# Row entries by distance from the middle of a row's span, and two seams of layer 0 in another order

## The chip, the cores and the metric

The kernel runs on one core of one Trainium2 chip. The metric is device time in microseconds of one execution; a profile of one execution shows what each engine did in it. The engines are named as in the profile: PE is TensorE (PEld its weight loads), DVE is VectorE, ACT is ScalarE, POOL is GpSimd, SP is SyncE, which here only issues DMAs.

## The reference, cut to what matters

Four graph layers run over x, 32 batches of 512 nodes with 128 features, and one adjacency matrix adj of 512 by 512. Each layer normalises x, applies a relu and adds the layer's output to x. The change lies in layer 0:

```python
h = jnp.maximum(_layernorm(x, axis=-1), 0.0)
# _L0_gnn_ref(h, adj, W, e, bias):
h0 = jnp.einsum('bnf,fg->bng', input, W[0])
h1 = jnp.einsum('bnf,fg->bng', input, W[1])
m = adj > 0
idx = jnp.cumsum(m.reshape(-1).astype(jnp.int32)) - 1
vals = e[0][idx].reshape(adj.shape)
A = jnp.where(m, vals, jnp.float32(NEG))
A = jax.nn.softmax(A, axis=1)
M = jnp.eye(adj.shape[0], dtype=A.dtype)
out = jnp.einsum('ij,bjg->big', A * M, h0) + jnp.einsum('ij,bjg->big', A * (1.0 - M), h1)
return out + bias[None, None, :]
```

The edges of adj are numbered row by row. Edge number k takes the k-th value of e, which has 256 entries; every edge beyond takes the last one. So the kernel has to find, for each of the first 256 edge numbers, the row and column that it lies in. A softmax over each row gives the attention matrix, whose diagonal multiplies h W[0] and whose other entries multiply h W[1].

## The kernel before

**Tiling.** The 512 rows of adj are four tiles (t = 0 to 3) of 128 partitions. The 32 batches are 16 pairs, q = 0 to 15, and x of a pair is one tile of 128 partitions by 2 by 4 by 128. All layers run pair by pair.

**The order of the work.** From by_source on, the instructions of TensorE, VectorE, ScalarE and GpSimd keep the order in which the source emits them, engine by engine. The emission is interleaved by hand: helpers are Python generators that emit some instructions per step, and go(steps, n) takes n steps of one. An instruction that waits holds all that stands behind it on its engine. DMAs are issued by SP; those under keep_in_program_order keep their order there too.

**The front (0 to about 15 us).** m is adj > 0 and rc[p, t] the number of edges in a row (L519). p_incl, a triangle of ones times rc (L528), is the number of edges up to and including a row; incl is its copy and before is incl - rc. Then edge k belongs to a row if before <= k < incl. The loop over t at L552 makes of_row[:, t, k] for k = 0 to 255 with two VectorE instructions: lt is k < incl (L554), and of_row is (k >= before) * lt (L555). TensorE multiplies each t with m into p_row (L558); its two banks go to pgs, one on ScalarE (L569) and one on VectorE (L570). p_upto is pgs times the triangle (L602), and scr_c (L616) counts from it the column of each edge. at_row, at_col and at_part (L619 to L623) are one-hot matrices; score_rows multiplies them into the score and value of each row tile (L654, L658), and softmax_rows and scaled_rows finish the attention matrix.

Beside it the statistics of x run for the first pairs: bn_stats on VectorE (L229), sd, sh and rs on GpSimd (L233 to L237), and h on ScalarE (L313).

**The seams.** In layer 0 each pair q goes through: statistics; h (normalise, eight ACTIVATEs at L313); hT, the transpose of h; p_g = hT times W[1] (L446, project_steps); g_high, g_low and g_mid, three parts of it (L468 to L474); p_l, the attention matrix times the parts (L800, mixed) plus own_sums, hd times W[0] (L793), where hd is hT times the diagonal (L728, GpSimd); and added (L808), which adds p_l to x. bias(q) adds the layer's bias to x on GpSimd (L453). For q up to 2, TensorE transposes h. From q = 3 on, turn(q) does it: two block transposes on VectorE (hb_hT, L349), four DMAs to DRAM (d_hT, L356) and one back (hT, L358), all issued on SP.

first_sums covers pair 0 and prepares pairs 1 to 3. Its first seam is at its end, where bias(1) stands ahead of the end of ln3, the statistics of pair 3 (the last two steps of which are L259 and L260 on GpSimd, the shift that h of pair 3 waits for):

```python
        diagonal_of(1, 1)
        bias(1)
        go(ln3)
        for I in range(2):
            added(0, I, ps[I])
```

round0(q) is the round of each later pair; it projects pair q + 1, turns pair q + 3 and starts h of pair q + 4. In round 2 alone the projection of pair 3 comes after mixed(q, 0). There lies the second seam: go(steps) emits p_g's evictions, and bias(q + 1) follows it, both ahead of turn(q + 3), which is turn(5). Loads of x for later pairs (load_x, L135) follow at the end of odd rounds.

Of the kernel before, what the change touches and what calls it, by code (L numbers as in the profile page):

```python
# [9 lines left out]
F32 = mybir.dt.float32  # L10
# [3 lines left out]
AF = mybir.ActivationFunctionType  # L14
OP = mybir.AluOpType
AX = mybir.AxisListType

P = 128
# [11 lines left out]
def kernel(  # L30
# [37 lines left out]
    nc = tc.nc  # L68
    B, N, D = x.shape
    NT = N // P  # L70
    NE = e_l0.shape[1]
    NK = NE // P
    NQ = B // 2
# [10 lines left out]
    def bank(name):  # L84
        return psum.tile([P, 512], F32, tag="bank", name=name)
# [4 lines left out]
    def blk(t):  # L90
        return slice(t * P, (t + 1) * P)
# [56 lines left out]
    def spread(w, n):  # L148
        return w[:, None, :].to_broadcast([P, n, D])
# [32 lines left out]
    prep = prep_scope.enter_context(tc.tile_pool(name="prep", bufs=1))  # L182
# [4 lines left out]
    cols = prep.tile([P, N], F16, name="cols")  # L187
# [118 lines left out]
    def normed_tile(q):  # L306
        return work.tile([P, 2, NT, D], F32, tag="h", name=f"h_{q}", bufs=3)
# [36 lines left out]
    def turn_steps(h, name, done):  # L344


        hb = late.tile([P, NQR, 2, NT, QR], F32, tag="hb", name=f"hb_{name}", bufs=2)
        for b in range(2):
            nc.vector.transpose(hb[:, :, b].rearrange("p j t r -> p t j r"),  # L349
                                h[:, b].rearrange("p t (j c) -> p t j c", c=QR))  # L350
            yield
        d = bounce.tile([NQR, QR, NQR, 2 * P], F32, tag="d", name=f"d_{name}")
        hT = feature_major(name)
        held = tc.keep_in_program_order if name.startswith("hT0") else lambda step: step
        for i in range(NQR):
            held(nc.sync.dma_start(d[:, :, i, :].rearrange("j c e -> c j e"),  # L356
                                   hb[i * QR : (i + 1) * QR].rearrange("c j b t r -> c j (b t r)")))
        held(nc.sync.dma_start(hT.rearrange("p i b n -> p (i b n)"), d.rearrange("j c i e -> (j c) (i e)")))  # L358
        done[name] = hT
# [90 lines left out]
    def bias(q):  # L450

        for b in range(2):
            nc.gpsimd.tensor_add(xt[q][:, b], xt[q][:, b], spread(b0, NT))  # L453
# [23 lines left out]
    def go(steps, n=99):  # L477
        for _ in range(n):
            if next(steps, steps) is steps:
                return  # L480
# [32 lines left out]
    rc = prep.tile([P, NT], F32, name="rc")  # L513
# [8 lines left out]
    rch = prep.tile([P, NT], F16, name="rch")  # L522
    nc.vector.tensor_copy(rch, rc)

    pi = bank("p_incl")
    for t in range(NT):
        for s in range(t + 1):
# [11 lines left out]
        nc.tensor.matmul(scores[t], ident16, m[:, t, :], start=True, stop=False)  # L539
    early = [early_stats(0, (0, 2), (2, 4)), early_stats(1, (0, 4)), early_stats(2, (0, 4))]  # L540
    go(early[0], 2)
    incl = prep.tile([P, NT], F32, name="incl")
    nc.vector.tensor_copy(incl, pi[:, :NT])
    before = prep.tile([P, NT], F32, name="before")
    nc.vector.tensor_sub(before, incl, rc)
    h = {q: normed_tile(q) for q in range(3)}
    hT = {q: feature_major(f"hT0_{q}") for q in range(3)}
    normal = [normed_steps(q, h[q]) for q in range(3)]
# [1 line left out]
    of_row = prep.tile([P, NT, NE], F16, name="of_row")  # L550
    pg = [bank(f"p_row_{i}").rearrange("p (j k) -> p j k", j=2) for i in range(NT // 2)]
    for t in range(NT):  # L552
        s = prep.tile([P, NE], F16, tag="lt", name=f"lt_{t}", bufs=2)
        nc.vector.tensor_scalar(s, cols[:, :NE], incl[:, t : t + 1], None, OP.is_lt)  # L554
        nc.vector.scalar_tensor_tensor(of_row[:, t, :], cols[:, :NE], before[:, t : t + 1], s,  # L555
                                       OP.is_ge, OP.mult)
        for j in range(NT):
            nc.tensor.matmul(pg[j // 2][:, j % 2, :], m[:, t, blk(j)], of_row[:, t, :],  # L558
                             start=(t == 0 and j % 2 == 0), stop=(t == NT - 1), skip_group_check=True)
    go(early[0], 2)  # L560
    nc.vector.tensor_scalar(known[:, :, 0], before, float(NE), None, OP.min)
    pb = bank("p_known")[:, : 2 * NK].rearrange("p (k e) -> p k e", e=2)
    for kk in range(NK):
# [50 lines left out]
    for kk in range(NK):  # L614
        s = prep.tile([P, N], F16, tag="scr", name=f"scr_c{kk}", bufs=2)
# [109 lines left out]
    def straight(hT, b, scale, name):  # L725

        s = owns.tile([P, N], F32, tag="hs", name=name, bufs=6)
        nc.gpsimd.tensor_mul(split(s), hT[:, :, b, :].rearrange("p b (a c) -> p a b c", c=QR), split(scale))  # L728
        return s
# [30 lines left out]
    ln3 = stats_steps(3, apart=True)  # L760
# [7 lines left out]
    def turn(q):  # L768

        if q not in turning:  # L770
            turning[q] = turn_steps(h[q], f"hT0_{q}", hT)
        next(turning[q])
        return turning[q]

    def turned_of(q):
        return hT[f"hT0_{q}"] if q > 2 else hT[q]
# [4 lines left out]
    def diagonal_of(q, b):  # L781
        hd[q, b] = straight(turned_of(q), b, adiag[0], f"hd_{q}_{b}")
# [13 lines left out]
    def mixed(q, I, p, part, first):  # L796

        for i in range(2):
            for t in range(NT):
                nc.tensor.matmul(p[:, i * 2 * D : (i + 1) * 2 * D], att_parts[part][:, t, blk(2 * I + i)],  # L800
                                 g[q][part][:, t].rearrange("p b f -> p (b f)"),
                                 start=(first and part == 0 and i == 0 and t == 0), stop=(part == 2 and t == NT - 1),
                                 skip_group_check=True)
# [6 lines left out]
    def first_sums():  # L810


        adiag.append(region0.tile([P, N], F32, name="adiag", bufs=1))
        ps = opened_sums(0)
        mixed(0, 0, ps[0], 0, True)
        transpose_rows(pt, att, 2)
        transpose_rows(pt, att, 3)
        for j in range(NT):
            att_high(j, 1, True)
        go(normal[1])  # L820
        go(early[2], NT + 2)
        att_low(1)
        att_mid(1)
        mixed(0, 0, ps[0], 1, True)
        mixed(0, 0, ps[0], 2, True)
        p_adiag = bank("p_adiag")
        for t in range(NT):
            nc.tensor.matmul(p_adiag[:, blk(t)], ones, diag[:, t, :], start=True, stop=True)
        nc.scalar.copy(adiag[0], p_adiag)
        go(early[2])  # L830
        diagonal_of(0, 0)
        diagonal_of(0, 1)
        next(turned[1])
        mixed(0, 1, ps[1], 0, True)
        go(turned[1])
        go(normal[2], NT)
        go(ln3, NT)
        next(project[1])
        mixed(0, 1, ps[1], 1, True)
        mixed(0, 1, ps[1], 2, True)  # L840
        go(project[1])
        go(normal[2])
        go(ln3, 1)
        own_sums(0, ps, False)
        diagonal_of(1, 0)
        diagonal_of(1, 1)
        bias(1)
        go(ln3)
        for I in range(2):
            added(0, I, ps[I])  # L850
        next(turned[2])
        go(turned[2])
        normalise(3)
        diagonal_of(2, 0)
        diagonal_of(2, 1)
        go(ahead[4], NT)
        go(turn(3))
        go(ahead[4])
# [3 lines left out]
    def round0(q):  # L862

        more = q + 1 < NQ
        nothing = iter(())
        both = stats_of_two(q - 1, q + 5) if q + 5 < NQ else stats_steps(q - 1, apart=True)
        ps = opened_sums(q)
        own_sums(q, ps, True)
        normal_of = normals.pop(q + 3, nothing)
        go(normal_of)  # L870
        go(both, NT)
        if more:
            if q > 1:
                diagonal_of(q + 1, 0)
                diagonal_of(q + 1, 1)
            steps = projection(q + 1)
            if q != 2:
                next(steps)
                if q > 2:
                    bias(q + 1)  # L880
                go(steps)
        if q + 5 >= NQ:
            go(both)
        if q == 1:
            bias(2)
            normalise(4)
            go(ahead[5])
            h[5] = normed_tile(5)
            normals[5] = normed_steps(5, h[5])
        elif q + 4 < NQ:  # L890
            h[q + 4] = normed_tile(q + 4)
            normals[q + 4] = normed_steps(q + 4, h[q + 4])
            go(normals[q + 4], NT)
        if q >= 5:
            go(sums_ahead, 1)
        for part in range(3):
            mixed(q, 0, ps[0], part, False)
        if q == 2:
            go(steps)
            bias(q + 1)  # L900
        if q + 3 < NQ:
            go(turn(q + 3))
        go(both, NT + 1)
        added(q, 0, ps[0])
        go(both)
        if q in (3, 4):
            next(squares)
            next(squares)
        if q == 5:
            go(squares)  # L910
        for part in range(3):
            mixed(q, 1, ps[1], part, False)
        added(q, 1, ps[1])
        if q == NQ - 1:
            own[q] = stats_steps(q)
        if q % 2 and q // 2 + NQ // 4 < NQ // 2:
            loads(q // 2 + NQ // 4)
# [613 lines left out]
```

## Time and profile before

| | |
|---|---|
| median of 3 runs | 883.40 us (883.37, 883.40, 884.81) |
| profiled execution: its own time | 883.62 us |
| its span, first to last instruction | 881.8 us |
| busy PE, PEld | 870.2 us (99%), 771.3 us (87%) |
| busy DVE, ACT, POOL | 702.4 us (80%), 574.7 us (65%), 608.4 us (69%) |
| granted TensorE clock, mean | 0.997 |

The profiled execution lies 0.2 us above the median. Its span leaves out 1.8 us around the first and the last instruction. Busy shares are means over four layers with different limits; what a change to layer 0 is worth has to be read from the stretches in which it lies, which are 7 to 15 us for the row entries and 40 to 76 us for the seams. Matmul ends are modelled in a trace, so TensorE counts as busy in some of its short waits; the starts of the weight loads show them better.

### The profile page before, as it was taken

To read this page: it belongs to the slowest core of one execution; us is meant where nothing else is said; L and a number is where in the kernel's file an instruction comes from. 1 tells how busy PE (TensorE), PEld (TensorE's weight loads), DVE (VectorE), ACT (ScalarE), POOL (GpSimd) and SP (SyncE) were. 2 spreads that over 40 slices of the span, in tenths; PEclk is the share of its full clock that TensorE was granted. 3 is DMA by queue.
4 is the path that set the end of the run, shared out by engine and by line. 5 is a ranking of instruction groups with operands and counts; after the bars stand their busy time and mean duration, and the time that the engine had idled before them with its cause. 6 is when DMAs were issued, how large, how long until landed. Compare 5 with 4: busy or idle time off the path is not lost.

```text
span 881.8 us, 16286 instructions
## 1 busy us (share of the span) xinstructions
PE 870.2 (99%) x5520; PEld 771.3 (87%) x5520; DVE 702.4 (80%) x1428; ACT 574.7 (65%) x1279; POOL 608.4 (69%) x624
## 2 busy tenths in 40 slices
PE   8999999999999999999999999999999999999998
PEld 4799999988888888888888888888889988899987
DVE  8769877568587787888778888888789789988875
ACT  4765565355555656556666888875688788766674
POOL 5768988766777867867776566565476766677664
PEclk9999999999999999999999999999999999999999
DMA  9146664312322213122342445455445555555433
GB/s 262 29 133 182 194 186 120 97 49 73 101 68 73 72 48 96 49 72 72 97 120 77 116 134 136 138 152 146 134 123 141 157 156 159 151 143 147 128 100 86
DMA packets 107684, 103.91 MB, mean 118 GB/s; under 512 B 9552, under 2 KB 94160, under 8 KB 107600
## 3 DMA queue, kind: packets, MB, share of 16 engines
q1 hardware_dynamic: 107312, 102.34, 41.1%
q8 instruction: 44, 0.72, 0.4%
q10 hardware_dynamic: 288, 0.52, 0.2%
q14 instruction: 40, 0.33, 0.1%
HBM read 53.02 MB, written 49.81 MB: 117 GB/s over the span
## 4 chain that ended last, share of the span: by engine, by line
PE 90%; DVE 3%; ACT 2%; POOL 2%; DMA 1%; issue 1%; SPq 0%; POOLq 0%; ACTq 0%; DVEq 0%
PE p_av L1298 13%; PE p_l L990 10%; PE p_hidden L1194 10%; PE p_x1T L397 10%; PE p_score L1276 10%; PE p_l L800 8%; PE p_w L969 5%; PE p_l L446 3%; PE p_z L446 3%; PE p_w L971 3%; PE p_feat L1171 3%; PE p_hidden L1174 3%; PE p_g L446 2%; PE p_query L1230 2%; PE p_hv L1242 2%; PE p_l L793 2%
## 5 line engine op out<-in xcount | busy, mean ns | idle before, releaser
L1298 PEld LDWEIGHTS p_av<-hv,ex 128*128 128x128 f32 x1024 | 119.2, 191 | 3.0 <-POOL ex L1271 0.4
L1298 PE MATMUL p_av<-hv,ex 128*128 128x129 f32 x1024 | 119.7, 274 | 0.2 <-POOL ex L1271 0.2
L313 ACT ACTIVATE h<-x,sh,rs 128x128 f32<-128x128 f32 x256 | 102.9, 483 | 4.4 <-POOL sh L260 2.3
L427 POOL TENSOR_TENSOR key<-key 128x512 fp32r<-128x512 f32 x32 | 47.9, 1498 | 83.4 <-DVE key L426 66.5
L1271 DVE TENSOR_TENSOR ex<-ex,adjTx 128x512 f32<-128x512 f32 x64 | 79.0, 1237 | 32.4 <-ACT ex L1269 31.0
L1271 POOL TENSOR_TENSOR ex<-ex,adjTx 128x512 f32<-128x512 f32 x64 | 99.6, 1574 | 6.9 <-issue 3.5
L1100 ACT ACTIVATE h<-x,sh,rs 128x128 f32<-128x128 f32 x256 | 102.9, 485 | 0.0
L413 POOL TENSOR_TENSOR low_h<-h,high_h 128x512 fp32r<-128x512 f32 x32 | 55.3, 1732 | 45.6 <-PE p_w L971 26.3
L1277 ACT ACTIVATE ex<-p_score 128x512 f32<-128x512 f32 x128 | 76.2, 598 | 11.5 <-PE p_score L1276 4.7
L1269 ACT ACTIVATE ex<-ex 128x512 f32<-128x512 f32 x128 | 77.3, 634 | 0.0
L1158 POOL TENSOR_SCALAR high_hT<-hT 128x512 fp32r<-128x512 f32 x32 | 20.5, 641 | 56.0 <-PE p_hidden L1174 28.9
L246 DVE BATCH_NORM_STATS2 bn<-x 128x6 f32<-128x256 f32 x160 | 58.3, 419 | 0.0
L399 ACT COPY x1T<-p_x1T 128x512 f32<-128x512 f32 x32 | 18.8, 587 | 57.7 <-PE p_x1T L397 57.7
L1214 POOL TENSOR_TENSOR x<-x,phi2b 128x256 f32<-128x256 f32 x64 | 56.3, 900 | 0.0
L413 POOL TENSOR_TENSOR low_hs<-hs,high_hs 128x512 fp32r<-128x512 f32 x32 | 44.0, 1388 | 14.9 <-ACT high_hs L412 14.4
L1276 PE MATMUL p_score<-high_query,key 128*128 128x512 f32 x128 | 50.5, 394 | 0.0
L1276 PE MATMUL p_score<-mid_query,key 128*128 128x512 f32 x128 | 50.4, 394 | 0.0
L1276 PE MATMUL p_score<-low_query,key 128*128 128x512 f32 x128 | 50.4, 394 | 0.0
L431 ACT ACTIVATE high_query<-p_query 128x512 fp32r<-128x512 f32 x32 | 19.2, 600 | 46.5 <-PE p_query L1230 46.5
L971 PE MATMUL p_w<-th,x1T 128*128 128x128 f32 x256 | 49.0, 273 | 0.0
L414 DVE SCALAR_TENSOR_TENSOR mid_h<-h,high_h 128x512 fp32r<-128x512 f32 x32 | 27.7, 870 | 23.7 <-ACT high_h L412 16.2
L1109 DVE STREAM_TRANSPOSE hb<-h 128x512 f32<-128x512 f32 x64 | 43.5, 697 | 2.5 <-DMA d<-hb 1.9
(246 smaller groups left out, 2623.1 us busy)
## 6 DMA issues: line engine op xcount, KB each, us to landing
d<-hb SPq DMA_DIRECT2D x128, 128.0 KB, 2.4
hT<-d SPq DMA_DIRECT2D x32, 512.0 KB, 3.7
d_hT<-hb_hT SPq DMA_DIRECT2D x116, 128.0 KB, 2.4
hT<-d_hT SPq DMA_DIRECT2D x29, 512.0 KB, 3.3
x<-in_x_dram SPq DMA_DIRECT2D x32, 256.0 KB, 5.3
dv<-hvb SPq DMA_DIRECT2D x128, 64.0 KB, 1.8
hvt<-dv SPq DMA_DIRECT2D x32, 256.0 KB, 2.7
out_dram<-x SPq DMA_DIRECT2D x31, 256.0 KB, 2.5
```

What stands on the lines that cost most here:

```text
L313: nc.scalar.activation(h[:, b, t, :], xt[q][:, b, t, :], AF.Relu, bias=shift[q][:, i : i + 1], scale=scale[q][:, i : i + 1])
L397: nc.tensor.matmul(p, right[part][:, blk(t)], left[part][:, t, :], start=(t == 0 and part == 0), stop=(t == NT - 1 and part == 2))
L413: nc.gpsimd.tensor_sub(low, x, high.bitcast(F32))
L971: nc.tensor.matmul(p[:, D:], x1[q, b][:, blk(t)], th[:, 2, :], start=False, stop=True, skip_group_check=True)
L990: nc.tensor.matmul(p, adj_parts[part][:, t, blk(i)], w[r][part][:, t, :], start=(part == 0 and t == 0), stop=(part == 2 and t == NT - 1))
L1100: nc.scalar.activation(h[:, t, :], xt[q][:, b, t, :], AF.Relu, bias=shift[q][:, i : i + 1], scale=scale[q][:, i : i + 1])
L1194: nc.tensor.matmul(sums2[n], weighed_features[n][i][:, blk(t)], sq[i][:, t, :], start=False, stop=(i == 2 and t == NT - 1), skip_group_che ...
L1269: nc.scalar.activation(ex[:, t, :], ex[:, t, :], AF.Exp, scale=8.0)
L1271: eng.tensor_mul(split(ex[:, t, :]), split(ex[:, t, :]), crossed(mask[:, t, :]))
L1276: nc.tensor.matmul(p, keys[n][i][:, t, :], query[n][i], start=(i == 0), stop=(i == 2))
L1277: nc.scalar.activation(crossed(ex[:, t, :]), split(p), AF.Tanh, scale=UP / (8.0 * math.sqrt(D)))
L1298: nc.tensor.matmul(po[:, i, : D + 1], ex[:, t, blk(i0 + i)], hv[:, t, :], start=(t == 0), stop=(t == NT - 1))
```

## The change

**Row entries.** The span of a row, before to incl - 1, has its middle at incl - rc/2 - 1/2. An edge number k lies in the row if its distance from the middle is less than rc/2. On GpSimd, half = rc/2 and above = rc/2 + 1/2 are made once for all t. middle = above - p_incl (VectorE, read from PSUM) is the middle with its sign turned. For each t, ScalarE makes s = |k + middle| (an ACTIVATE of function Abs with a bias per partition), and VectorE makes of_row = s < half. The copy incl is gone, and before is made after the loop, from PSUM.

**Two seams.** In first_sums, go(ln3) now stands ahead of bias(1). In round0, turn(q + 3) now stands ahead of the projection's evictions of round 2; for other rounds the emission is the same.

TensorE's and SP's instructions keep their order. VectorE has four instructions fewer, ScalarE four more, GpSimd two more.

```diff
     rch = prep.tile([P, NT], F16, name="rch")
     nc.vector.tensor_copy(rch, rc)
 
+    half = prep.tile([P, NT], F32, name="half")
+    nc.gpsimd.tensor_scalar(half, rc, 0.5, None, OP.mult)
+    above = prep.tile([P, NT], F32, name="above")
+    nc.gpsimd.tensor_scalar(above, rc, 0.5, 0.5, OP.mult, OP.add)
+
...
     go(early[0], 2)
-    incl = prep.tile([P, NT], F32, name="incl")
-    nc.vector.tensor_copy(incl, pi[:, :NT])
-    before = prep.tile([P, NT], F32, name="before")
-    nc.vector.tensor_sub(before, incl, rc)
+    middle = prep.tile([P, NT], F32, name="middle")
+    nc.vector.tensor_sub(middle, above, pi[:, :NT])
...
         s = prep.tile([P, NE], F16, tag="lt", name=f"lt_{t}", bufs=2)
-        nc.vector.tensor_scalar(s, cols[:, :NE], incl[:, t : t + 1], None, OP.is_lt)
-        nc.vector.scalar_tensor_tensor(of_row[:, t, :], cols[:, :NE], before[:, t : t + 1], s,
-                                       OP.is_ge, OP.mult)
+        nc.scalar.activation(s, cols[:, :NE], AF.Abs, bias=middle[:, t : t + 1])
+        nc.vector.tensor_scalar(of_row[:, t, :], s, half[:, t : t + 1], None, OP.is_lt)
...
     go(early[0], 2)
+    before = prep.tile([P, NT], F32, name="before")
+    nc.vector.tensor_sub(before, pi[:, :NT], rc)
     nc.vector.tensor_scalar(known[:, :, 0], before, float(NE), None, OP.min)
...
         diagonal_of(1, 1)
+        go(ln3)
         bias(1)
-        go(ln3)
         for I in range(2):
...
             mixed(q, 0, ps[0], part, False)
+        if q + 3 < NQ:
+            go(turn(q + 3))
         if q == 2:
             go(steps)
             bias(q + 1)
-        if q + 3 < NQ:
-            go(turn(q + 3))
         go(both, NT + 1)
```

## The prediction

> **What bounds the kernel now.** I read the chain of waits first, then TensorE's own waits, then the timeline around each wait. The page's chain is TensorE nearly throughout, so a change counts only where TensorE stands still or where another engine feeds it late:
>
> ```profile
> PE 90%; DVE 3%; ACT 2%; POOL 2%; DMA 1%; issue 1%; SPq 0%; POOLq 0%; ACTq 0%; DVEq 0%
> ```
>
> Both seams lie in layer 0. TensorE's waits between 20 and 140 us (total us, times, longest) hold one DMA row, met twice:
>
> ```profile
> PE p_g L446 <- DMA hT<-d_hT: 1.5, 2, 1.2
> ```
>
> The timeline of weight loads (start, duration) shows their full price, because load starts have a fixed pitch: a part of eight p_l L800 matmuls starts 0.96 us after the last, and p_g L446 follows sixteen L793 loads after 1.80 us (62.61 to 64.41):
>
> ```profile
> 56.47 1.03 PEld L800 LDWEIGHTS p_l<-g_mid,att_mid 128*128 128x128 f32 x8
> 57.96 1.86 PEld L446 LDWEIGHTS p_g<-w,hT 128*128 128x128 f32 x16 [0.47 <-issue]
> ...
> 62.61 1.88 PEld L793 LDWEIGHTS p_l<-w,hd 128*128 128x128 f32 x16
> 64.41 1.87 PEld L446 LDWEIGHTS p_g<-w,hT 128*128 128x128 f32 x16
> ...
> 71.94 1.88 PEld L793 LDWEIGHTS p_l<-w,hd 128*128 128x128 f32 x16
> 75.22 1.86 PEld L446 LDWEIGHTS p_g<-w,hT 128*128 128x128 f32 x16 [1.40 <-DVE bn L272]
> ```
>
> p_g of batch pair 3 was due at 56.47 + 0.96 = 57.43 and starts at 57.96: 0.53 lost. p_g of pair 5 was due at 71.94 + 1.80 = 73.74 and starts at 75.22: 1.48 lost. Together 2.01 us.
>
> The same timeline, all engines, shows why hT arrives late:
>
> ```profile
> 43.57 2.51 POOL L453 TENSOR_TENSOR x<-x,b 128x512 f32<-128x512 f32 x2
> 46.38 0.20 POOL L260 TENSOR_TENSOR sh<-sh,rs 128x8 f32<-128x8 f32 x1
> 46.61 3.20 ACT L313 ACTIVATE h<-x,sh,rs 128x128 f32<-128x128 f32 x8 [2.30 <-POOL sh L260]
> ...
> 58.46 4.72 ACT L313 ACTIVATE h<-x,sh,rs 128x128 f32<-128x128 f32 x12
> 63.69 1.29 DVE L470 SCALAR_TENSOR_TENSOR g_low<-g_high,p_g 128x512 fp32r<-128x512 f32 x2 [2.84 <-ACT g_high L468]
> 65.49 1.30 DVE L349 STREAM_TRANSPOSE hb_hT<-h 128x512 f32<-128x512 f32 x2
> 66.81 1.77 SPq L356 DMA_DIRECT2D d_hT<-hb_hT  x4
> 71.85 0.34 SPq L358 DMA_DIRECT2D hT<-d_hT  x1
> ```
>
> First seam: bias(1) holds GpSimd 2.51 us while the shift of pair 3 stands behind it; ScalarE idles 2.30 us, and everything to hT_3 is that late. Second seam: h_5 is the first 8 of the 12 ACTIVATEs at 58.46, yet its transposes stand on VectorE behind g_low, which idles VectorE 2.84 us waiting for ScalarE.
>
> The front: VectorE alternates four lt and four of_row, while ScalarE waits for GpSimd's statistics.
>
> ```profile
> 8.15 0.28 DVE L554 TENSOR_SCALAR lt<-cols,incl 128x256 f16<-128x256 f16 x1
> 10.62 0.48 DVE L555 SCALAR_TENSOR_TENSOR of_row<-cols,before,lt 128x256 f16<-128x256 f16 x1
> 9.99 0.46 POOL L237 TENSOR_TENSOR sh<-sh,rs 128x4 f32<-128x4 f32 x1
> 10.48 0.88 ACT L313 ACTIVATE h<-x,sh,rs 128x128 f32<-128x128 f32 x2 [1.52 <-DMA w<-in_L_gnn_W_dram]
> 11.57 0.59 ACT L569 CAST pgs<-p_row 128x512 f16<-128x512 f32 x1 [0.22 <-PE p_row L558]
> ```
>
> The DMA named before h is doubtful: L237 ends at 10.45, h starts at 10.48.
>
> **What the skill says.** The Trainium skill, "ScalarE: Activation LUTs", *What ACT_TABLE_LOAD costs*: an ACTIVATE with a pointer bias takes 280 ns + 0.833 ns per column, each further pointer about 93, and neighbours overlap by about 93. The trace agrees: h (two pointers, 128 columns) works out at 480 ns, measured 484; the exp at L668 (bias, 512 columns) at 706, measured 722. *Table sets: the hidden batching unit* puts abs into every set, so no table load is added; no run so far shows an Abs. "TensorE: Matmul & The Clock Gate", *What's actually happening*: too quiet a window halves TensorE's clock for windows of 3413 ns that run free of the kernel. Here the granted clock is 0.54 at 30 to 31 us, 0.50 until 33 and 0.76 until 34: one such window.
>
> **Seam 1** (go(ln3) ahead of bias(1)). No instruction is added or removed; on GpSimd the two small L259 and L260 pass the two L453. L260 needs rs of L257, ready at 43.08, so both can run from 43.6 when hd_1 ends. h_3 then waits only for ScalarE's hT copies, which end at 44.31: it starts at about 44.24 (overlap), 2.37 earlier. Its transposes and DMAs follow; no other SP entry lies between. hT_3, which now releases TensorE at 57.96, lands near 55.6, 1.8 before it is due. Saved: the whole 0.53. Cost: bias(1) and hd_2 are pushed back about 0.5 at most; hd_2 ended at 49.07 and its first reader, own_sums(2), loads at 52.77, so 3.7 us cover it. added(1), which needs bias(1), comes at 58.12 on VectorE.
>
> **Seam 2** (turn(5) ahead of project(3)'s evictions). On VectorE the two L349 transposes (1.30) pass two g_low and a g_mid. On the old clock h_5 is done at 58.84 + 7 × 0.39 + 0.1 = 61.7 (0.39 is the pitch of L313; a gap before 58.84 is in the chain), the transposes at 62.9: inside the 2.84 us in which VectorE idled, so g_low stays at 63.69. SP then issues four d_hT after its x loads (61.10 + 2.08 = 63.18) in place of 66.81: 3.6 earlier, and with seam 1 another 2. No SP entry changes place; it is the x loads' traffic that d_hT_5 meets sooner. The waiting transposes hold g_low behind them, but ScalarE does h_5 before g_high, so never longer than their own 1.3 us; the low part is read at 67.14 and ready at 64.98, 2.2 us of cover. hT_5 took 8.3 us from first issue to TensorE's start (66.81 to 75.1); the worst like case, pair 9 behind x and adjT loads, was issued at 101.88, with its last leg at 108.37 and 3.3 to land: 9.8. From 63.2 this is 73.0 at the worst, while TensorE, 0.53 earlier, is due at 73.21. Saved: the whole 1.48.
>
> What is late next: hT_6 is issued at 77.70 and lands in 3.3 at 81.0, due at 84.65 - 2.0; hT_9 lands at 111.7, due at 112.6, and its SP queue starts from VectorE work that follows p_g, so it moves along. From about 95 us VectorE and ScalarE wait for p_g each round, so the lead reaches the end: 2.01 us.
>
> **Front.** Removed from VectorE: incl, 4 lt (0.28) and the two-input of_row (0.48). A lt and of_row pair takes 0.72 by its starts (8.15, 8.87, 9.59, 10.31), and the last of_row ends at 11.10. Added: half and above on GpSimd, 4 Abs on ScalarE; of_row becomes one tensor_scalar of lt's shape, 0.28.
> - GpSimd: att ends at 8.00; half and above, 0.25 each like L233 and L234 (0.23, 0.24), end about 8.55. middle (0.17) then ends at 8.76, against incl at 8.04.
> - ScalarE: an Abs of 256 columns is 280 + 213 = 493 ns, pitch 400 (estimates from the skill; L376 without pointer 0.37). First Abs at 8.88, after qkT. lt has two buffers, so the third waits for the first of_row (9.41 to 9.69) and starts at 9.73, the fourth at 10.13 to 10.62. The last of_row ends at 10.94: 0.16 gained, and p_row with VectorE's pgs too.
> - Against it: sd, sh, rs stand 0.5 later on GpSimd, so h_0 starts at 11.0 in place of 10.48, and ScalarE's pgs at 11.8 in place of 11.57. p_upto thus starts 0.2 later (12.43) and its first bank is ready near 13.17. VectorE's scr_c, at 13.20 before and free from 13.04, starts at 13.17.
>
> before = p_incl - rc now follows the last of_row, in the 0.60 us that VectorE waits for p_row ahead of pgs: nothing.
>
> Net -0.03, held by whichever is later. The later hT copy (0.2) is hidden: p_val waits for the six at_part on VectorE anyway. Bounds: -0.4 if GpSimd and Abs are as quick as L376, +0.6 if the Abs and of_row hand-overs do not overlap.
>
> **Sum.** -0.53 - 1.48 - 0.03 = -2.04 against the profiled execution's 883.62 (span 881.8 and 1.8 around it): 881.58. The median of the runs is 883.40, 0.22 less: **881.4**, or 0.23% faster. A measurement here tells about 0.2%, 1.77 us, from no change, so the forecast lies just beyond that line.
>
> **Rivals.**
> - *Front loses what it shifts to GpSimd and ScalarE.* For: h_0 and pgs are in order behind the Abs, and ScalarE's slack before pgs was only 0.22. Against: VectorE gains 0.16 at the same join. +0.3 to +1.0: about 882.0. Chance 0.14.
> - *A DMA wait takes the place of the order wait.* d_hT_5 now meets the x loads; if hT_5 is still late by 0.5 to 1.5 us, 882.5. For: 73.0 against 73.21 if seam 1 passes nothing on. Against: seam 1 moves this chain 2 us. Chance 0.08.
> - *The clock, ending slower.* The half clock at 30 us lies where transposes and p_l are fed late. Work that moves against the free windows can meet more of it between 26 and 45 us: each added window costs 3.4 × 0.5 = 1.7 us. It decides from 4.1 us of added half clock; two windows give 881.4 + 3.4 = 884.8, three 886.5. For: the runs before spread by 1.4. Against: the clock is 1.00 from 34 us to the end. Chance 0.10, half of it three windows.
> - *More gain*: front at its lower bound, 880.9. Chance 0.06. That the change does not do what it says is excluded: the order of each engine shows the moves and no added table load.
>
> **Numbers.** The likeliest case has 0.62, with its own range 880.9 to 881.9; a tenth of it falls inside 0.2%. Faster: 0.56 + 0.06 = 0.62. Same: 0.06 + 0.14 + 0.08 + 0.05 (one or two windows) = 0.33. Slower by over 0.2%: 0.05, from three windows. 880.5 to 883.0 leaves out most of the clock and part of the DMA case.
>
> **What would show it.** Right: no wait of p_g for hT near 56 and 72 us; L260 before L453; L349 ahead of L470 in that round; four Abs of about 0.49 and no third table load. Wrong: p_g still waiting after hT_5's DMA, pgs on ScalarE later than 12.1, or granted clock under 1 beyond 34 us.

## The result and the profile after

The changed kernel takes **881.95 us** (median of 12 runs, 881.22 to 883.40). The kernel before, run beside it, takes 883.64 us (12 runs, 883.29 to 884.81). The ratio is 0.998 (95% interval 0.9972 to 0.9987), 1.69 us or 0.19% less; the interval lies wholly below 1. Beside the later experiments it ran again, under the label e7_changed_again, and gave 0.9971 (0.9961 to 0.9981). The profiled execution took 882.33 us with a span of 880.5 us, against 883.62 and 881.8 before.

The page's chain of waits has lost its DMA share, and TensorE holds 95% of it instead of 90%:

```profile
PE 95%; DVE 2%; POOL 1%; ACT 1%; issue 1%; POOLq 0%; ACTq 0%; DVEq 0%
```

TensorE's own waits from 20 to 140 us (total us, times, longest) no longer hold the row of p_g after the DMA hT:

```profile
PE p_l L804 <- DVE att_high L378: 0.8, 1, 0.8
PE p_attT L485 <- DVE att_mid L390: 0.6, 1, 0.6
PE p_attT L485 <- POOL att L683: 0.3, 1, 0.3
```

The timeline of weight loads (start, duration) shows both p_g parts on the pitch, 0.96 us after the p_l part of pair 1 and 1.79 us after the sixteen loads of hd. No idle stands in brackets:

```profile
57.16 1.03 PEld L804 LDWEIGHTS p_l<-g_mid,att_mid 128*128 128x128 f32 x8
58.12 1.87 PEld L446 LDWEIGHTS p_g<-w,hT 128*128 128x128 f32 x16
...
72.11 1.88 PEld L797 LDWEIGHTS p_l<-w,hd 128*128 128x128 f32 x16
73.90 1.87 PEld L446 LDWEIGHTS p_g<-w,hT 128*128 128x128 f32 x16
```

p_g of pair 3 starts 0.16 us later than before (58.12 for 57.96), p_g of pair 5 1.32 us earlier (73.90 for 75.22). Two waits worth 2.01 us are gone and the lead is 1.32 us, which the span keeps to its end (1.3 us). Something took about 0.7 us back ahead of 58 us. The timeline of ScalarE narrows it down; the first line is of before, the second of after:

```profile
35.49 0.59 ACT L829 COPY adiag<-p_adiag 128x512 f32<-128x512 f32 x1
...
36.18 0.59 ACT L833 COPY adiag<-p_adiag 128x512 f32<-128x512 f32 x1 [0.71 <-PE p_adiag L832]
```

The clock by stretches of 1 us points to the reason (columns: stretch, its sum, TensorE's busy time with its instructions, granted clock, DMA share, GB/s). In the changed kernel:

```profile
28.00:29.00 1.00, 1.00 (x6) 0.67 0.03 8
29.00:30.00 1.00, 0.41 (x2) 0.50 0.00 0
...
33.00:34.00 1.00, 1.00 (x7) 0.50 0.00 0
34.00:35.00 1.00, 1.00 (x6) 0.50 0.00 0
35.00:36.00 1.00, 1.00 (x11) 0.92 0.00 0
```

In the kernel before, the first and the last stretch with a lower clock:

```profile
30.00:31.00 1.00, 1.00 (x4) 0.54 0.00 0
...
33.00:34.00 1.00, 1.00 (x8) 0.76 0.00 0
```

The half clock lasted from about 28.3 to 35.2 us, where the profile of before has it from 30.1 to 33.5. That is two windows of 3.4 us for one. The copy adiag, the first reader of TensorE behind it, came at 36.18 us for 35.49. The front itself was 0.08 us early (scr_c at 13.12 for 13.20), so the clock, if it is the cause, cost 0.69 + 0.08 = 0.77 us. Then -0.08 + 0.77 - 2.01 = -1.32, and the spans differ by -1.3. An experiment below sets the clock by hand.

The runs agree with this. One window at half clock loses 3.4 × 0.5 = 1.7 us of an 880 us span, or 0.002 of the mean clock. Six of the 12 runs have a mean clock of 0.998 or more and took 881.22 to 881.74 us. The other six have 0.996 and took 882.17 to 883.40.

### The profile page after: what moved, and what is told of

Read it like the earlier page. It is cut to its first block, busy times and chain, and to the rows that moved or that the text cites. A ratio compares the mean times of both kernels' runs of the same rounds, so it can differ in the third digit from the quotient of the medians.

```text
span 880.5 us, 16289 instructions
## 1 busy us (share of the span) xinstructions
PE 871.0 (99%) x5520; PEld 772.3 (88%) x5520; DVE 700.9 (80%) x1424; ACT 576.3 (65%) x1283; POOL 608.9 (69%) x626
## 4 chain that ended last, share of the span: by engine, by line
PE 95%; DVE 2%; POOL 1%; ACT 1%; issue 1%; POOLq 0%; ACTq 0%; DVEq 0%
PE p_av L1302 13%; PE p_l L804 10%; PE p_l L994 10%; PE p_hidden L1198 10%; PE p_x1T L397 10%; PE p_score L1280 10%; PE p_w L973 5%; PE p_l L797 3%; PE p_l L446 3%; PE p_z L446 3%; PE p_g L446 3%; PE p_w L975 3%; PE p_feat L1175 3%; PE p_hidden L1178 3%; PE p_query L1234 2%; PE p_hv L1246 2%
## 5 line engine op out<-in xcount | busy, mean ns | idle before, releaser
L432 DVE SCALAR_TENSOR_TENSOR z<-p_z,z 128x512 fp32r<-128x512 f32 x31 | 21.4, 691 | 30.3 <-ACT z L431 30.3
```

## The experiments

Each is compared with runs of the kernel before on the same chip. That median was 884.07 us for the first four, 884.25 for the next two, and 884.13 for the last three.

### Parts of the change

**Both seams on the old front.** The edit is the two diffs shown below for the first and the second seam, together.

> The kernel before with both seams moved and its row entries left as they were. Theory A (the seams are worth the full 2.01 us, the row entries nothing, and what is missing of the gain is half clock between 28 and 36 us): no wait of p_g for hT in the trace, p_g of pairs 3 and 5 on pitch (0.96 and 1.80 us after the part ahead), and a median 1.5 to 2.0 us under the kernel before, the same as the whole change within 0.3 us. Theory B (the row entries cost about 0.3 us that the seams give): 0.3 us or more faster than the whole change. Theory C (the row entries bring a part of the gain): at most 1.4 us under the kernel before.

Measured: 882.17 us (881.36 to 883.46), ratio 0.9973 (0.9965 to 0.9982). Its profile, of the slowest of the 12 runs, again has two half-clock windows, 28 to 34.8 us, and both p_g parts on the pitch.

**Row entries alone,** on the old seams:

```diff
-        nc.vector.tensor_scalar(s, cols[:, :NE], incl[:, t : t + 1], None, OP.is_lt)
-        nc.vector.scalar_tensor_tensor(of_row[:, t, :], cols[:, :NE], before[:, t : t + 1], s,
-                                       OP.is_ge, OP.mult)
+        nc.scalar.activation(s, cols[:, :NE], AF.Abs, bias=middle[:, t : t + 1])
+        nc.vector.tensor_scalar(of_row[:, t, :], s, half[:, t : t + 1], None, OP.is_lt)
```

> The kernel before with the new row entries and both seams left as they were. Theory A: within 0.2 us of the kernel before in the median; p_g still waits for hT near 58 and 75 us; scr_c starts within 0.1 us of before, measured from the end of the last m. Theory B: 0.3 us or more slower. Theory C: 0.3 us or more faster.

Measured: 884.05 us (883.62 to 885.29), ratio 0.9999 (0.9991 to 1.0008). The row entries are worth nothing that can be measured, and the waits for hT stay. Weight loads of this kernel:

```profile
58.04 1.86 PEld L446 LDWEIGHTS p_g<-w,hT 128*128 128x128 f32 x16 [0.25 <-issue]
...
75.57 1.86 PEld L446 LDWEIGHTS p_g<-w,hT 128*128 128x128 f32 x16 [1.67 <-DVE bn L272]
```

**The first seam alone:**

```diff
         diagonal_of(1, 1)
+        go(ln3)
         bias(1)
-        go(ln3)
```

> The kernel before with go(ln3) ahead of bias(1) alone. If the two seams add up as the prediction had them (0.53 and 1.48): 0.5 us faster, and p_g of pair 5 starts 1.9 to 2.0 us late after pitch. If the first seam also pulls hT_5 along (pair 3's chain moves all of VectorE's and ScalarE's work up to h_5 by 1.7 us): 1.5 to 1.8 us faster, with 0.2 to 0.5 us of wait left at pair 5.

Measured: 881.81 us (881.42 to 882.63), ratio 0.9972 (0.9964 to 0.9981). **One seam has the whole gain** that can be measured, and the second wait is gone too although nothing was done to it. Its p_g of pair 5 is on the pitch, 1.80 us after the loads of hd at 71.76:

```profile
71.76 1.88 PEld L793 LDWEIGHTS p_l<-w,hd 128*128 128x128 f32 x16
73.56 1.87 PEld L446 LDWEIGHTS p_g<-w,hT 128*128 128x128 f32 x16
```

VectorE's part of the timeline shows that the transposes of pair 5 still stand behind g_low, but that both are about 2 us earlier:

```profile
61.62 1.28 DVE L470 SCALAR_TENSOR_TENSOR g_low<-g_high,p_g 128x512 fp32r<-128x512 f32 x2 [2.86 <-ACT g_high L468]
63.42 1.30 DVE L349 STREAM_TRANSPOSE hb_hT<-h 128x512 f32<-128x512 f32 x2
```

SP's queue of the same kernel shows what follows from them:

```profile
64.75 1.77 SPq L356 DMA_DIRECT2D d_hT<-hb_hT  x4
68.62 0.34 SPq L358 DMA_DIRECT2D hT<-d_hT  x1
```

d_hT is issued at 64.75 us, 2.06 earlier than before, and its last leg, the load of hT back, at 68.62, 3.23 earlier; from the one to the other take 3.87 us for 5.04. In the changed kernel, with the second seam as well, d_hT is issued another 2.43 us earlier, and the last leg only 0.31:

```profile
60.19 2.08 SPq L135 DMA_DIRECT2D x<-in_x_dram  x4
62.32 2.43 SPq L356 DMA_DIRECT2D d_hT<-hb_hT  x4
68.31 0.34 SPq L358 DMA_DIRECT2D hT<-d_hT  x1
```

From the first issue to the last leg it takes 5.99 us there. What VectorE wins is spent behind the loads of x; that they also slow the transfer itself is likely, but was not tried by itself.

**The second seam alone:**

```diff
+        if q + 3 < NQ:
+            go(turn(q + 3))
         if q == 2:
             go(steps)
             bias(q + 1)
-        if q + 3 < NQ:
-            go(turn(q + 3))
```

> The kernel before with turn(5) ahead of the evictions alone. By the prediction's terms: the wait of pair 3 stays (0.53 us) and the one of pair 5 goes, 1.4 to 1.5 us faster. If hT_5 is then held by the x loads' traffic (rival of the DMA wait): 0.5 to 1.2 us faster, with a wait of p_g for hT_5 still in the trace.

Measured: 883.42 us (881.76 to 884.89), ratio 0.9991 (0.9983 to 0.9999). By the medians that is 0.65 us, less than half of its 1.48; the interval reaches from about 0.1 to 1.5 us. TensorE's waits, its weight loads and SP's queue, in a profile of the slowest of its 13 runs (884.89 us):

```profile
PE p_g L446 <- DMA hT<-d_hT: 0.7, 2, 0.4
```

```profile
72.91 1.88 PEld L793 LDWEIGHTS p_l<-w,hd 128*128 128x128 f32 x16
75.37 1.86 PEld L446 LDWEIGHTS p_g<-w,hT 128*128 128x128 f32 x16 [0.59 <-DVE bn L272]
```

```profile
62.02 2.08 SPq L135 DMA_DIRECT2D x<-in_x_dram  x4
64.15 3.88 SPq L356 DMA_DIRECT2D d_hT<-hb_hT  x4
71.97 0.34 SPq L358 DMA_DIRECT2D hT<-d_hT  x1
```

p_g of pair 5 was due at 72.91 + 1.80 = 74.71 us and starts at 75.37, still 0.66 late. d_hT is issued 2.66 us earlier than before, right behind the x loads, but its last leg goes out at 71.97 for 71.85: it takes 7.8 us for 5.0. This is the prediction's DMA rival, met where the first seam does not stand ahead. With both seams the same way took 5.99 us, and 7.68 in the second profile of the changed kernel (e7_changed_again), and p_g did not wait in either. In the profile of before that rival has no line, because there the transposes come too late to collide.

### The clock

The two clusters above are an observation. To set the clock by hand, 14 matmuls without use were put where TensorE waits in first_sums; what they write is overwritten by the matmuls that follow. The rest of the source is as it was.

```diff
         ps = opened_sums(0)
+        for i in range(6):
+            nc.tensor.matmul(ps[0][:, :D], hT[0][:, i % NT, 0, :], w0[:, 1, :], start=True, stop=True)
         mixed(0, 0, ps[0], 0, True)
+        for i in range(8):
+            nc.tensor.matmul(ps[1][:, : 2 * D], att_parts[0][:, i % NT, blk(0)],
+                             g[0][0][:, i % NT].rearrange("p b f -> p (b f)"), start=True, stop=True)
         transpose_rows(pt, att, 2)
```

**In the changed kernel:**

> The changed kernel with 14 matmuls more on TensorE, whose results are overwritten: 6 of w0 and hT_0 while it waits for att_high at 26 us, 8 of att_high and g_high while it waits for att_mid at 28 us. Theory A (half clock in free-running windows after a too quiet one sets the spread of the changed kernel): granted clock 1.0 from 20 us to the end in nearly every run, runs within 0.5 us of each other, median at about 881.4, 0.3 to 0.8 us under the changed kernel, and p_adiag done near 35.4 us in place of 36.2. If the half clock costs nothing on the path: the median stays where it is (within 0.2 us) though the clock is full. If the added matmuls stand in the way: 0.5 us or more slower, with att_high or the second transposes later.

Measured: 881.28 us (5 runs, 881.24 to 881.57), ratio 0.9964 (0.9952 to 0.9977). The clock is 1.00 in every stretch from 26 to 40 us:

```profile
29.00:30.00 1.00, 1.00 (x7) 1.00 0.00 0
30.00:31.00 1.00, 0.99 (x8) 1.00 0.00 0
31.00:32.00 1.00, 1.00 (x11) 1.00 0.00 0
```

The spread shrinks from 2.2 us in 12 runs to 0.33 in 5. Together with the two clusters this puts most of the spread of the changed kernel down to the clock; another source of spread shows further below. p_g of pair 5 starts at 72.85 us for 73.90.

**In the kernel before:**

> The kernel before with the same 14 matmuls more, results overwritten. Theory A: full clock; its most frequent case had one half-clock window that was hidden behind ScalarE's h, so its median moves by 0 to 0.3 us only, and the runs of 884.4 and more are gone. If the half clock costs nothing: nothing changes, and the spread of 1.5 us stays.

Measured: 883.77 us (21 runs, 882.90 to 885.72), ratio 0.9996 (0.9989 to 1.0002), with the clock at 1.00 in the profile too. The medians differ by 0.48 us, which the interval cannot tell from nothing, and the spread stays. TensorE's waits, its weight loads and SP's queue for pair 3, in a profile of one of the slower runs (885.04 us):

```profile
PE p_g L446 <- DMA hT<-d_hT: 2.3, 2, 1.6
```

```profile
59.10 1.86 PEld L446 LDWEIGHTS p_g<-w,hT 128*128 128x128 f32 x16 [1.76 <-issue]
```

```profile
50.55 3.01 SPq L356 DMA_DIRECT2D d_hT<-hb_hT  x4
55.48 0.34 SPq L358 DMA_DIRECT2D hT<-d_hT  x1
```

TensorE is due at this p_g only 0.16 us earlier than before (57.27 for 57.43), and d_hT is issued 0.16 us earlier (50.55 for 50.71). The wait is longer because the transfer is slower: its last leg goes out at 55.48 us for 54.52. Why it is slower in this run is open. So in this profile the full clock moved the chain by 0.16 us, as little as is expected if one half-clock window hides behind ScalarE's h.

That the kernel before pays nothing for the half clock does not follow. Of its 79 runs beside the experiments, the 12 with a mean clock of 1.0 took 883.12 to 883.84 us, and the 29 with 0.995 or 0.996 took 884.41 to 886.03. A lower clock thus goes with about 1 us more there as well. With the clock full the runs of 884.4 and more were expected to be gone, but five of the 21 are there: part of the spread has another source.

**The changed kernel once more,** beside the two that follow, is the same code as above.

> The changed kernel itself, on the same chip as the two runs with added matmuls beside it. If half clock sets its spread: two clusters again, near 881.5 (at most one half-clock window, mean clock 0.998 or more) and near 882.5 (two windows, mean clock 0.996), 1.5 to 2.3 us under the kernel before in the median.

Measured: 881.74 us (881.35 to 882.39), ratio 0.9971 (0.9961 to 0.9981). The profile has one half-clock window, about 29.4 to 32.8 us. The clusters show again, unevenly: seven runs have a mean clock of 0.998 and took 881.35 to 881.98 us, one has 0.996 and took 882.39.

**The first seam and the 14 matmuls on the kernel before.** The edit is the two diffs together.

> The kernel before with go(ln3) ahead of bias(1) and the 14 added matmuls (results overwritten); old row entries, turn(5) where it was. If the first seam carries the whole gain and the clock the whole spread: 881.2 to 881.5, runs within 0.5 us, the same as the changed kernel with the 14 matmuls (881.28). If the second seam is needed once TensorE runs at full clock and so reaches pair 5 sooner: 0.3 to 0.8 us slower than that, with a wait of p_g for hT_5.

Measured: 881.65 us (881.37 to 882.80), ratio 0.9972 (0.9962 to 0.9983). p_g has no wait for hT. The spread was expected within 0.5 us and is 1.4. The profile, of the slowest run (882.80 us; the other seven lie between 881.37 and 881.94), shows where that run lost its time: at 427 us, far behind layer 0, VectorE's mid_hT (L1166) took 1.84 us and TensorE's weight load waited 1.19 us for it. The first line is of the profile of the first seam alone, where the same instruction took 0.68:

```profile
427.59 0.68 DVE L1161 SCALAR_TENSOR_TENSOR mid_hT<-hT,high_hT 128x512 fp32r<-128x512 f32 x1
...
427.39 1.84 DVE L1166 SCALAR_TENSOR_TENSOR mid_hT<-hT,high_hT 128x512 fp32r<-128x512 f32 x1
...
429.28 0.19 PEld L1176 LDWEIGHTS p_feat<-mid_hT,w_low 128*128 128x128 f32 x1 [1.19 <-DVE mid_hT L1166]
```

Of the 11 profiles, 7 have 0.68 us for this instruction and 4 have 1.84 to 1.86, whatever the seams and the clock: both seams on the old front, the second seam alone, the 14 matmuls in the kernel before, and this one. Those four profiled runs are the slowest, or among the three slowest, of their kernels. So there is a second source of spread of 1.1 to 1.2 us besides the clock. No run tries its cause. The median is no better than that of the seam alone (881.81), and why is open.

### A quicker front

The changed front has three holds that its profile shows. middle waits for above on GpSimd; the first Abs stands behind the copy qkT; the third Abs waits for a free lt buffer. On top of the changed kernel with the 14 matmuls, this kernel takes all three away at once, so their shares are not known apart:

```diff
-    nc.gpsimd.tensor_scalar(half, rc, 0.5, None, OP.mult)
+    nc.vector.tensor_scalar(half, rc, 0.5, None, OP.mult)
...
-    nc.gpsimd.tensor_scalar(above, rc, 0.5, 0.5, OP.mult, OP.add)
+    nc.vector.tensor_scalar(above, rc, 0.5, 0.5, OP.mult, OP.add)
...
-    nc.scalar.copy(qkT, tiles(p)[:, :2, :])
...
-        s = prep.tile([P, NE], F16, tag="lt", name=f"lt_{t}", bufs=2)
+        s = prep.tile([P, NE], F16, tag="lt", name=f"lt_{t}", bufs=NT)
...
+    nc.scalar.copy(qkT, tiles(p)[:, :2, :])
```

> The changed kernel with the 14 matmuls (results overwritten) and a quicker front: half and above on VectorE, qkT's copy behind the four Abs on ScalarE, four lt buffers in place of two. If the row entries brought nothing because middle waits for above, Abs for qkT's copy and the third Abs for a buffer: the first Abs at about 8.3 us, the last of_row done near 10.4 in place of 11.0, ScalarE's pgs near 11.0 in place of 11.5, and 0.4 to 0.6 us faster than the changed kernel with the 14 matmuls. If the front is held elsewhere (GpSimd's queue, the second x batch): within 0.2 us of it.

Measured: **880.88 us** (5 runs, 880.79 to 881.07), ratio 0.9965 (0.9952 to 0.9977). It beats both kernels: 3.25 us under the kernel before and 0.86 under the changed one beside it, 0.4 of it over the 14 matmuls alone, with ranges that don't touch (881.24 to 881.57 there). That step of 0.4 us rests on these times and on the traces: the two kernels ran on different chips, and their ratios to the runs of before beside each do not differ (0.9965 and 0.9964). In the timeline the four Abs start 0.50 us earlier than with the 14 matmuls alone (8.76), run at a pitch of 0.40, and of_row follows without a break:

```profile
8.26 1.70 ACT L556 ACTIVATE lt<-cols,middle 128x256 f16<-128x256 f16 x4 [5.11 <-DVE middle L547]
...
8.80 1.48 DVE L557 TENSOR_SCALAR of_row<-lt,half 128x256 f16<-128x256 f16 x4 [0.64 <-ACT lt L556]
...
12.57 0.74 DVE L620 TENSOR_SCALAR_CACHE_REDUCE scr_c<-p_upto,rest 128x512 f16<-128x512 f32 x1
```

scr_c starts 0.43 us earlier than with the 14 matmuls alone (13.00), and p_g of pair 5 0.42 earlier (72.43 for 72.85). Here, where no later wait of p_g stands behind it, the gain of the front reaches the end almost whole. The quick front was not tried in the kernel before, so no run shows that the waits would have hidden it there.

## Why the prediction was right, and where it was wrong

**The total was near, the sum behind it partly wrong.** Forecast was -2.04 us and 881.4; measured are -1.69 and, in the later comparison, -2.39. That p_g stands still for hT at two places, that both waits go and that the lead reaches the end is shown by the waits and weight loads of after.

**The first seam's place was right, its size too small.** GpSimd's two small instructions pass the bias, and ScalarE starts h of pair 3 right behind them. The timeline of after:

```profile
44.28 0.25 POOL L259 TENSOR_SCALAR sh<-bn 128x8 f32<-128x8 f32 x1
44.61 0.20 POOL L260 TENSOR_TENSOR sh<-sh,rs 128x8 f32<-128x8 f32 x1
44.77 2.51 POOL L453 TENSOR_TENSOR x<-x,b 128x512 f32<-128x512 f32 x2
44.89 3.19 ACT L313 ACTIVATE h<-x,sh,rs 128x128 f32<-128x128 f32 x8
```

h starts at 44.89 us where 44.24 was forecast; the clock's 0.69 at adiag accounts for that. But its share in the sum was 0.53 us, and alone it brought 2.26 (884.07 - 881.81).

**The step that failed is the addition: "Saved: the whole 1.48" for the second seam on top of the first.** The prediction saw that seam 1 moves the chain to hT of pair 5 by 2 us, and used it only as reserve for a collision. Those 2 us alone cover a wait of 1.48. The second wait was thus the tail of the first delay, not a second one. The total for the two together stands, since both waits go; the shares do not. With the first seam done the second adds nothing that can be measured (882.17 with both, 881.81 with one), and without it, it brought 0.65 by the medians.

**The front was forecast at -0.03, and nothing of it can be measured** (0.9999). The steps held within 0.1 us for the Abs: first at 8.89 us (forecast 8.88), the four in 1.77, each 0.49 to 0.51, which agrees with the price that the prediction took from the Trainium skill, "ScalarE: Activation LUTs", *What ACT_TABLE_LOAD costs*. No table load is added: the kernel has three in all, before and after, and not two, as "no third table load" has it. The last of_row ended at 10.98 (10.94), scr_c started at 13.12 (13.17). One step was wrong and cost nothing: h of pair 0 was to start at 11.0 us and ScalarE's pgs at 11.8, and they start at 10.57 and 11.50, as the last section shows.

**Rivals.** The front's loss did not come. The DMA wait did not take the place of the order wait with both seams, and did with the second alone. The clock came partly: one more window, in about half of the runs. But a window was priced at 1.7 us, and the two clusters lie 0.9 apart (medians 881.50 and 882.42), which agrees with a part of a window falling where TensorE stands still anyway (0.41 busy at 29 to 30 us). One sign of being wrong that the prediction named did come, a granted clock under 1 beyond 34 us (0.50 from 34 to 35 us in the profile). It meant one more window, 0.77 us in that profile, and not the 4.1 us of added half clock that were to decide.

## What to carry to other kernels

Where two waits stand in one chain, ask of the later one how late it would be if the earlier delay were gone, before adding the two. After a wait is removed, look again at what lies ahead of it: in the changed kernel a full clock and a quicker front each took about 0.4 us more off the median, though the runs do not show that the old waits had hidden it. An instruction that is moved to let a transfer start earlier gains only as much as the transfers in front of it leave over.

## What was not expected of the hardware

**The half clock varies from run to run and can be filled away.** The same code had one window (29.4 to 32.8 us) or two (28.3 to 35.2). The Trainium skill, "TensorE: Matmul & The Clock Gate", *What's actually happening*, says that windows of 3.4 us run free of the kernel, with which both lengths agree; it lets the clock come back after a busy window. 14 small matmuls in the gaps kept it at 1.00 from 26 to 40 us in all four kernels profiled with them.

**GpSimd's small operations got shorter when VectorE did less.** rs (L236, 128x4) took 1.04 us for 1.32 before, and sh (L237) 0.20 for 0.46. The first line is of before:

```profile
8.59 1.32 POOL L236 TENSOR_TENSOR rs<-sd,minus_half 128x4 f32<-128x4 f32 x1
...
8.88 1.04 POOL L236 TENSOR_TENSOR rs<-sd,minus_half 128x4 f32<-128x4 f32 x1
9.99 0.20 POOL L237 TENSOR_TENSOR sh<-sh,rs 128x4 f32<-128x4 f32 x1
```

sd stands 0.34 us later on GpSimd than before, yet sh starts at 9.99 us in both kernels, so the half and above ahead of it cost h nothing. In the kernel before, sh ran from 9.99 to 10.45 us, and VectorE's of_row with two inputs from 9.90 to 10.38 beside it; after, VectorE's of_row has one input, ends its second at 10.11 and starts its third at 10.30. The Trainium skill, "SBUF — State Buffer", *SBUF: two separate sides*, says that GpSimd and VectorE share a pair of ports, and that a VectorE operation with two inputs in SBUF can hold it against GpSimd for its whole length. The times agree with that; no run here tried it by itself.
